# Column buffers and turned images in the second layer of a convolution-and-GRU kernel

## The chip, the cores and the metric

The kernel runs on one core of one Trainium2 chip. The metric is device time in microseconds of one execution; the time of the kernel before is the median of three runs, 5828.33 us (5819.98 to 5828.91). The core's engines are TensorE (PE in the profile, its weight loads PEld), VectorE (DVE), ScalarE (ACT), GpSimd (POOL) and SyncE (SP), which here only issues DMAs.

## The reference

Two layers, each added to its input, each on the group-normalized input (`_gn`, over 32 groups of channels):

```python
x = x + _L0_conv_ref(_gn(x), ...)   # 1x1 conv, depthwise 3x3, per-patch FFT product, layer norm, gate, 1x1 conv
x = x + _L1_conv_ref(_gn(x), ...)   # a GRU that walks over the columns of the image
```

All is float32, on a tensor of 4 images, 64 channels, 256 x 256 pixels. The change touches the second layer (layer 1) alone:

```python
f = jnp.transpose(features, (3, 0, 2, 1))            # columns first
def step(prev_col, cur_col):
    nb = jnp.concatenate([pad, prev_col, pad], axis=1)
    x = jnp.concatenate([nb[:, :-2], nb[:, 1:-1], nb[:, 2:]], axis=-1)   # three neighbours of the last new column
    new = _gru_cell(x, cur_col, w_ih, w_hh, b_ih, b_hh)                  # h = the old column
    return (new, new)
```

with r and z the sigmoids of the two gates, n = tanh(i_n + r * h_n), and the new column (1 - z) * n + z * h. Column 0 stays as it is; each of the 255 others needs the new column to its left, so the layer is a chain of 255 steps.

## The kernel before, in words

Layer 0 works block by block (32 blocks of 1024 patches), writes its result to a tensor in HBM (`x1`), and keeps its statistics on the chip. The change leaves its code alone. When its last store has landed, layer 1 begins.

In layer 1 a column of all four images is one tile of 128 partitions x 2 slots x 256 pixels: two images lie in the two halves of the partitions, two more in the second slot. The pairing of images with halves and slots differs between even and odd columns (`SLOTS`), because the matmuls of a step write the images into the other arrangement than the one that they read. An even column is one DMA, an odd one is two, one for each half.

- Loads. `load_columns(w)` (line 750) loads the columns w and w+1 by three DMAs on SP's queue, into `raw`, a tile of eight columns with three buffers (line 737). Sixteen columns are loaded ahead of the first step.
- Normalization. `normalize(w, slot)` (line 766) is an ACT instruction per slot that writes the normalized column into `xn`, a tile of eight columns with two buffers. The matmuls need two of the four images also in the other half of the partitions. After every second column, line 779 copies these from `xn` to `xt` by two DMAs from SBUF to SBUF on SP's queue. Nine columns are normalized ahead of the first step (line 877); step w then normalizes column w+8.
- A step. `column(w)` (line 819) cuts the 256 rows in two parts, whose border moves by one row per step and jumps back every 32 steps, so that part 0 of a step needs nothing of part 1 of the step before. For each part PE computes the gates into PSUM tiles: `pshr` (own column, then three taps of the last new column `st`), `pshn` (whole column, in part 0), `psni` (taps), `pshz` (own column and taps). `own` reads `xn` and `xt`. `state` (line 856) turns these into the new column: ACT makes g, z and n, DVE does five operations, of which the last writes `st`.
- Result. `add(w)` (line 785) is a GpSimd addition that puts the new column onto `raw` in place. After every second column three DMAs on SP's queue store both columns. Then three more load columns w+15 and w+16 (line 889).

The order on each engine is the order of the program (`InOrder`, lines 146 to 160); SP and GpSimd too work their queues in order. Tile pools put in the waits: a tile handed out again waits for all users of the buffer's last tile. Each DMA of SP takes one of eight completion semaphores in turn, and waits for the DMA that had it before.

Of the kernel before, what the change touches and what calls it, by code (L numbers as in the profile page):

```python
# [10 lines left out]
F32 = mybir.dt.float32  # L11
# [8 lines left out]
P = 128  # L20
# [143 lines left out]
def tile_conv_then_gru(  # L164
# [128 lines left out]
    with layer0 as s:  # L293
# [20 lines left out]
        def normalize(n, jq):  # L314

            t, b, at = xq[n, jq], n // 8, n % 8
            flat = t.rearrange("p j k -> p (j k)")
            shift, rstd = sc0[:, b, 0:1], sc0[:, b, 1:2]
            if jq == 3:
                nc.vector.tensor_scalar(flat, flat, rstd, shift, ALU.mult, ALU.add)  # L320
            else:
                nc.scalar.activation(flat, flat, AF.Identity, bias=shift, scale=rstd)
            grid = t.rearrange("p j (r c) -> p j r c", c=10)
            if jq % 2 == 0:
                nc.gpsimd.memset(grid[:, 0, :, 0:1], 0.0)
            else:
                nc.gpsimd.memset(grid[:, 15, :, 9:10], 0.0)
            if at == 0 and jq < 2:
                nc.gpsimd.memset(grid[0:C, :, 0, :], 0.0)
            if at == 7 and jq >= 2:  # L330
                nc.gpsimd.memset(grid[C:P, :, 9, :], 0.0)
# [402 lines left out]

    WB = 8
    with ExitStack() as s:
        rawp = s.enter_context(tc.tile_pool(name="raw", bufs=3))
        colp = s.enter_context(tc.tile_pool(name="cols", bufs=2))
        gk = s.enter_context(tc.tile_pool(name="gk", bufs=2))
        ps_g = s.enter_context(tc.tile_pool(name="ps_g", bufs=1, space=PSUM))  # L740
        raws, xns, xts, stcols = {}, {}, {}, {}

        def columns(m, w):

            yield m[:, :, w, :].rearrange("(k a) c h -> (a c) k h", k=NPAIR), slice(0, P), 0
            for half in range(2):
                b0 = SLOTS[1][0][half]
                yield m[b0 : b0 + 2, :, w + 1, :].rearrange("b c h -> c b h"), slice(half * C, half * C + C), 1

        def load_columns(w):  # L750
            n, i = w // WB, w % WB
            if i == 0:
                raws[n] = rawp.tile([P, 2, WB, H], F32, tag="raw", name=f"raw_{n}")
            for of, at, j in columns(x1, w):
                nc.sync.dma_start(raws[n][at, :, i + j], of)

        def new_columns(n):
            xns[n] = colp.tile([P, 2, WB, H], F32, tag="xn", name=f"xn_{n}")
            xts[n] = colp.tile([P, WB, H], F32, tag="xt", name=f"xt_{n}")

        def empty_states(n):
            stcols[n] = st = colp.tile([P, 2, WB, H + 2], F32, tag="st", name=f"st_{n}")
            nc.gpsimd.memset(st[:, :, :, 0:1], 0.0)
            nc.gpsimd.memset(st[:, :, :, H + 1 : H + 2], 0.0)

        def normalize(w, slot):
            n, i = w // WB, w % WB
            if i == slot == 0:
                new_columns(n)
            nc.scalar.activation(  # L770
                xns[n][:, slot, i],
                raws[n][:, slot, i],
                AF.Identity,
                bias=sc1[:, w % 2, slot, 0:1],
                scale=sc1[:, w % 2, slot, 1:2],
            )
            if slot and i % 2:

                for half in range(2):
                    nc.sync.dma_start(  # L780
                        xts[n][half * C : (half + 1) * C, i - 1 : i + 1],
                        xns[n][(1 - half) * C : (2 - half) * C, half, i - 1 : i + 1],
                    )

        def add(w):
            n, i = w // WB, w % WB
            nc.gpsimd.tensor_tensor(
                raws[n][:, :, i], raws[n][:, :, i], stcols[n][:, :, i, 1 : H + 1], ALU.add
            )
            if i % 2:  # L790
                for of, at, j in columns(out, w - 1):
                    nc.sync.dma_start(of, raws[n][at, :, i - 1 + j])

        QUARTERS = ((0, 0), (0, 1), (1, 0), (1, 1))
        SKEW = 32

        def parts(w):


            at = H // 2 + SKEW // 2 - (w - 1) % SKEW  # L800
            return (0, at), (at, H)

        MAX = H // 2 + SKEW // 2

        def bank_pair(gate, w):
            return ps_g.tile([P, 2, 512], F32, tag=gate, name=f"ps{gate}_{w}")

        def quarters(ps, weights, rhs, start, stop):
            for r, c in QUARTERS:
                nc.tensor.matmul(  # L810
                    ps[c * C : (c + 1) * C, r],
                    lhsT=weights[r * C : (r + 1) * C],
                    rhs=rhs(r, c),
                    start=start,
                    stop=stop,
                    tile_position=(r * C, c * C),
                )

        def column(w):

            i, xn, xt, st = w % WB, xns[w // WB], xts[w // WB], stcols[(w - 1) // WB]

            def own(ps, gate, h0, h1, stop):

                quarters(
                    ps,
                    wh[:, gate, :],
                    lambda r, c: (xn[:, c] if r == c else xt)[r * C : (r + 1) * C, i, h0:h1],
                    True,
                    stop,  # L830
                )

            def taps(ps, gate, h0, h1, start):
                for t in range(3):
                    quarters(
                        ps,
                        wi[:, 3 * gate + t, :],
                        lambda r, c: st[r * C : (r + 1) * C, c, (w - 1) % WB, h0 + t : h1 + t],
                        start and t == 0,
                        t == 2,  # L840
                    )

            pn = bank_pair("hn", w)[:, :, 0:H]
            for part in range(2):
                h0, h1 = parts(w)[part]
                pr, pi, pz = (bank_pair(gate, f"{w}_{part}")[:, :, 0 : h1 - h0] for gate in ("hr", "ni", "hz"))
                own(pr, 0, h0, h1, False)
                taps(pr, 0, h0, h1, False)
                if part == 0:
                    own(pn, 2, 0, H, True)  # L850
                taps(pi, 2, h0, h1, True)
                own(pz, 1, h0, h1, False)
                taps(pz, 1, h0, h1, False)
                state(w, part, pn[:, :, h0:h1], pr, pi, pz)

        def state(w, part, pn, pr, pi, pz):
            h0, h1 = parts(w)[part]
            i, num = w % WB, h1 - h0
            xn, st = xns[w // WB], stcols[w // WB]
            g = gk.tile([P, 2, MAX], F32, tag=f"g{part}", name=f"g_{w}_{part}")[:, :, 0:num]  # L860
            n = gk.tile([P, 2, MAX], F32, tag=f"n{part}", name=f"n_{w}_{part}")[:, :, 0:num]
            z = gk.tile([P, 2, MAX], F32, tag=f"z{part}", name=f"z_{w}_{part}")[:, :, 0:num]
            nc.scalar.activation(g, pr, AF.Sigmoid, bias=b_rz[:, 0:1], scale=1.0)
            if w + WB < W:
                normalize(w + WB, part)
            nc.vector.scalar_tensor_tensor(n, pn, bias_sb[:, 5:6], g, ALU.add, ALU.mult)
            nc.vector.tensor_tensor(n, pi, n, ALU.add)

            nc.scalar.activation(z, pz, AF.Sigmoid, bias=b_rz[:, 1:2], scale=-1.0)
            nc.scalar.activation(n, n, AF.Tanh, bias=bias_sb[:, 2:3], scale=1.0)  # L870
            nc.vector.scalar_tensor_tensor(g, z, -1.0, xn[:, :, i, h0:h1], ALU.add, ALU.mult)
            nc.vector.tensor_tensor(n, n, z, ALU.mult)
            nc.vector.tensor_tensor(st[:, :, i, 1 + h0 : 1 + h1], n, g, ALU.subtract)

        for w in range(0, 2 * WB, 2):
            load_columns(w)
        for w in range(WB + 1):
            for slot in range(2):
                normalize(w, slot)
        empty_states(0)  # L880
        nc.vector.tensor_copy(stcols[0][:, :, 0, 1 : H + 1], xns[0][:, :, 0])
        for w in range(W):
            n, i = w // WB, w % WB
            if i == 0 and n + 1 < W // WB:
                empty_states(n + 1)
            if w:
                column(w)
            add(w)
            if i % 2 and w + 2 * WB < W:
                load_columns(w + 2 * WB - 1)  # L890


# [59 lines left out]
```

## Time and profile before

| | before |
|---|---|
| median of the runs | 5828.33 us (5819.98 to 5828.91) |
| the profiled execution's own time | 5838.45 us |
| its span, first to last instruction | 5836.7 us, granted TensorE clock 0.993 |
| layer 0, from 0 to about 4303 us | PE busy 4069.9 us of 4303 |
| layer 1's steps, 4324 to 5830 us (1506 us) | PE busy 1401.2, PEld 1336.2, DVE 1059.7, ACT 906.5, POOL 306.8 us |
| DMA in this stretch | 41% of the time of 16 engines, 112 GB/s |

Layer 1 takes about a quarter of the time. Each row of the profile names the engine, the operation and the tiles that it writes and reads (out<-in); all rows carry line 158, the line of the helper through which each instruction is recorded, so the tiles are what to go by. Idle time is given with what ended it. "issue" there means that the profile shows no semaphore for which the engine waited. A busy PE isn't a PE at its peak, since matmuls overlap: the weight loads (PEld) show more sharply when PE's instruction stream stands still.

### The profile page before, as it was taken

The page shows a single profiled execution, that of the slowest core. Times are in us where ns is not written, and L with a number is a line of the kernel's source. Part 1 is how long each engine was busy: PE and PEld are TensorE (multiplying, and loading weights), DVE is VectorE, ACT ScalarE, POOL GpSimd, SP SyncE. Part 2 cuts the span into 40 slices and gives each one's busy share as a digit, 9 for nine tenths or more (in the row PEclk, how much of TensorE's full clock was granted, in tenths as well). Part 3 has the DMA queues.
Part 4 walks back from the last instruction along what each step waited for, and adds up shares of the span by engine and source line. Part 5 has one row for each costly group of instructions (what it writes and reads, how often), then busy time and mean ns, then how long its engine had stood idle before and what let it go on. Part 6 is the DMA issues. An engine that isn't in the chain of part 4 may idle for free. (4 is left out here: it accounts for less than half of the span.)

```text
span 5836.7 us, 278467 instructions
## 1 busy us (share of the span) xinstructions
PE 5472.7 (94%) x127204; PEld 4752.8 (81%) x127204; DVE 4076.5 (70%) x9593; ACT 3475.0 (60%) x4604; POOL 476.3 (8%) x749
## 2 busy tenths in 40 slices
PE   4999999999999999999999999999979999999998
PEld 3888888778878888888878888888768888888888
DVE  4777677777777777766777677666667776777766
ACT  3656666556566666556556666565556665666655
POOL 0000000000000000000000000000002221222212
PEclk9999999999999999999999999999989999999999
DMA  7555555555555555555555554544444444444443
GB/s 251 149 153 157 154 155 142 149 158 150 152 150 156 154 146 141 160 149 148 151 144 152 143 134 130 145 133 129 136 116 115 117 114 112 115 117 116 119 112 84
DMA packets 557274, 818.28 MB, mean 140 GB/s; under 512 B 37484, under 2 KB 431632, under 8 KB 553712
## 3 DMA queue, kind: packets, MB, share of 16 engines
q1 hardware_dynamic: 522256, 634.46, 40.4%
q0 software_dynamic: 33552, 165.43, 8.9%
q8 instruction: 996, 16.32, 1.2%
q14 instruction: 182, 1.49, 0.1%
q10 hardware_dynamic: 288, 0.58, 0.0%
HBM read 622.72 MB, written 144.05 MB: 131 GB/s over the span
## 5 line engine op out<-in xcount | busy, mean ns | idle before, releaser
L158 PEld LDWEIGHTS psring<-h,t 100*32 100x32 f32 x40960 | 1333.4, 115 | 303.9 <-issue 200.6
L158 PE MATMUL psring<-h,t 100*32 100x128 f32 x40960 | 1445.3, 274 | 115.3 <-issue 41.4
L158 PEld LDWEIGHTS psring<-w_sb,xq 64*100 64x100 f32 x24576 | 1355.8, 163 | 81.4 <-issue 51.1
L158 PE MATMUL psring<-w_sb,xq 64*100 64x128 f32 x24576 | 1399.9, 271 | 21.6 <-issue 7.6
L158 ACT COPY h<-psring 100x1024 f32<-100x1024 f32 x1274 | 1205.7, 1026 | 162.8 <-PE psring L158 154.4
L158 DVE TENSOR_TENSOR pr<-psring,q 128x512 f32<-128x512 f32 (+1 forms) x576 | 462.9, 857 | 336.5 <-PE psring L158 326.4
L158 DVE BATCH_NORM_STATS2 lnst<-z 128x6 f32<-128x64 f32 x4096 | 545.7, 216 | 117.6 <-ACT z L158 117.6
L158 DVE TENSOR_TENSOR z<-z,lnm 128x1024 f32<-128x1024 f32 x512 | 612.8, 1218 | 8.7
L158 ACT COPY q<-psring 128x1024 f32<-128x1024 f32 x256 | 259.3, 1013 | 527.4 <-PE psring L158 445.3
L158 ACT ACTIVATE z<-pshz,b_rz 128x288 f32<-128x288 f32 (+7 forms) x510 | 242.5, 476 | 520.6 <-PE pshz L158 520.6
L158 PE MATMUL pshr<-st,wi 64*64 64x144 f32 (+7 forms) x12240 | 511.2, 270 | 42.0 <-issue 26.1
L158 ACT COPY z<-psring 128x2048 f32<-128x2048 f32 x128 | 238.9, 1867 | 520.9 <-PE psring L158 520.9
L158 PE MATMUL pshz<-st,wi 64*64 64x144 f32 (+7 forms) x12240 | 513.0, 271 | 25.3 <-issue 24.0
L158 PE MATMUL psni<-st,wi 64*64 64x144 f32 (+7 forms) x12240 | 510.2, 270 | 21.0 <-issue 20.0
L158 PE MATMUL psring<-pr,g_sb 32*64 32x512 f32 x8192 | 488.7, 599 | 5.2 <-issue 5.1
L158 ACT ACTIVATE y<-psring,ln_sb 128x512 f32<-128x512 f32 x512 | 372.1, 780 | 201.5 <-PE psring L158 199.0
L158 PEld LDWEIGHTS psni<-st,wi 64*64 64x64 f32 x12240 | 447.1, 133 | 41.9 <-issue 30.1
L158 PEld LDWEIGHTS pshr<-st,wi 64*64 64x64 f32 x12240 | 422.2, 133 | 57.5 <-issue 54.8
L158 PEld LDWEIGHTS pshz<-st,wi 64*64 64x64 f32 x12240 | 427.0, 133 | 38.4 <-issue 37.7
L158 DVE COPY h<-psring 100x1024 f32<-100x1024 f32 x262 | 320.1, 1222 | 171.8 <-PE psring L158 167.9
L158 DVE SCALAR_TENSOR_TENSOR g<-z,xn 128x288 f32<-128x288 f32 (+7 forms) x510 | 218.4, 428 | 311.9 <-ACT z L158 310.3
L158 DVE TENSOR_TENSOR y<-psring,y 128x1024 f32<-128x1024 f32 x256 | 312.4, 1221 | 128.8 <-ACT y L158 127.9
(100 smaller groups left out, 7342.4 us busy)
## 6 DMA issues: line engine op xcount, KB each, us to landing
t<-t_all SPq DMA_DIRECT2D x768, 400.0 KB
xq<-in_xh POOLq DMA_DIRECT2D x128, 800.0 KB, 4.6
xr<-in_x SPq DMA_DIRECT2D x256, 256.0 KB
x<-xr SPq DMA_DIRECT2D x256, 256.0 KB
raw<-x SPq DMA_DIRECT2D x128, 256.0 KB
raw<-x SPq DMA_DIRECT2D x256, 128.0 KB
xt<-xn SPq DMA_DIRECT2D x256, 128.0 KB
out<-raw SPq DMA_DIRECT2D x128, 256.0 KB
```

The source lines that it names most:

```text
L158: return self.tc.keep_in_program_order(got(*args, **kwargs))
```

## The change

Columns get a buffer each: `raw` becomes a tile of one column with 16 buffers. After each step its column is stored at once, by one DMA (even) or two (odd), and one column is loaded, into the buffer that was just stored. The two images in `xt` are written by two GpSimd copies per column, in place of two DMAs per two columns. Four columns in place of nine are normalized ahead of the first step; steps 1 to 5 normalize two columns each, until the lead is eight columns as before.

```diff
-        rawp = s.enter_context(tc.tile_pool(name="raw", bufs=3))
+        rawp = s.enter_context(tc.tile_pool(name="raw", bufs=2 * WB))
...
-        def columns(m, w):
-
-            yield m[:, :, w, :].rearrange("(k a) c h -> (a c) k h", k=NPAIR), slice(0, P), 0
-            for half in range(2):
-                b0 = SLOTS[1][0][half]
-                yield m[b0 : b0 + 2, :, w + 1, :].rearrange("b c h -> c b h"), slice(half * C, half * C + C), 1
-
-        def load_columns(w):
-            n, i = w // WB, w % WB
-            if i == 0:
-                raws[n] = rawp.tile([P, 2, WB, H], F32, tag="raw", name=f"raw_{n}")
-            for of, at, j in columns(x1, w):
-                nc.sync.dma_start(raws[n][at, :, i + j], of)
+        def column_parts(m, w):
+
+            raw = raws[w]
+            if w % 2 == 0:
+                yield m[:, :, w, :].rearrange("(k a) c h -> (a c) k h", k=NPAIR), raw
+            else:
+                for half in range(2):
+                    b0 = SLOTS[1][0][half]
+                    yield m[b0 : b0 + 2, :, w, :].rearrange("b c h -> c b h"), raw[half * C : half * C + C]
+
+        def load_column(w):
+            raws[w] = rawp.tile([P, 2, H], F32, tag="raw", name=f"raw_{w}")
+            for of, to in column_parts(x1, w):
+                nc.sync.dma_start(to, of)
...
-                raws[n][:, slot, i],
+                raws[w][:, slot],
...
-            if slot and i % 2:
+            if slot:
 
                 for half in range(2):
-                    nc.sync.dma_start(
-                        xts[n][half * C : (half + 1) * C, i - 1 : i + 1],
-                        xns[n][(1 - half) * C : (2 - half) * C, half, i - 1 : i + 1],
+                    nc.gpsimd.tensor_copy(
+                        xts[n][half * C : (half + 1) * C, i], xns[n][(1 - half) * C : (2 - half) * C, half, i]
                     )
 
         def add(w):
-            n, i = w // WB, w % WB
-            nc.gpsimd.tensor_tensor(
-                raws[n][:, :, i], raws[n][:, :, i], stcols[n][:, :, i, 1 : H + 1], ALU.add
-            )
-            if i % 2:
-                for of, at, j in columns(out, w - 1):
-                    nc.sync.dma_start(of, raws[n][at, :, i - 1 + j])
+            nc.gpsimd.tensor_tensor(raws[w], raws[w], stcols[w // WB][:, :, w % WB, 1 : H + 1], ALU.add)
+            for to, of in column_parts(out, w):
+                nc.sync.dma_start(to, of)
...
-            if w + WB < W:
-                normalize(w + WB, part)
+            for more in range(ahead(w - 1), ahead(w)):
+                normalize(more, part)
...
-        for w in range(0, 2 * WB, 2):
-            load_columns(w)
-        for w in range(WB + 1):
+        def ahead(w):
+
+            return min(2 * w + 4, w + WB + 1, W)
+
+        for w in range(2 * WB):
+            load_column(w)
+        for w in range(ahead(0)):
             for slot in range(2):
                 normalize(w, slot)
...
         for w in range(W):
-            n, i = w // WB, w % WB
-            if i == 0 and n + 1 < W // WB:
-                empty_states(n + 1)
+            if w % WB == 0 and w + WB < W:
+                empty_states(w // WB + 1)
             if w:
                 column(w)
             add(w)
-            if i % 2 and w + 2 * WB < W:
-                load_columns(w + 2 * WB - 1)
+            if w + 2 * WB < W:
+                load_column(w + 2 * WB)
```

## The prediction

> **What bounds the kernel now.** The table of stretches comes first: layer 1's steps fill 1506 us, and PE is busy for 93% of them. The list of waits in that stretch says what the rest is.
>
> ```profile
> engine line waited for: us in total, times, longest us
> ...
> ACT z L158 <- PE pshz L158: 520.6, 510, 3.0
> ...
> PEld pshr L158 <- issue: 67.7, 95, 2.2
> ...
> PEld pshz L158 <- issue: 46.6, 76, 1.5
> ...
> PEld psni L158 <- issue: 30.1, 46, 1.5
> ...
> PE pshr L158 <- DVE st L158: 13.4, 7, 1.9
> ```
>
> ACT waits for PE, so PE sets the pace. PE itself waits for the recurrence (`st`) in 7 places alone, the jumps of the border. Its other pauses, 67.7 + 46.6 + 30.1 = 144 us, have no semaphore behind them. The chain of work shows them in the middle of a group of matmuls, here around 5242 us:
>
> ```profile
> 5241.77 0.47 PE psni L158 x16
> 5242.24 0.63 issue
> 5242.87 0.47 PE psni L158 x8
> ```
>
> The DMA table of the stretch says what comes in without a semaphore: instructions.
>
> ```profile
> q1 hardware_dynamic: 158638, 162.65, 39.6%
> q8 instruction: 366, 6.00, 1.7%
> ```
>
> 366 packets of 16,384 bytes in 1506 us, one per 4.1 us. I set these packets' records beside PE's and the data packets' records of the trace. A pause ends, nearly always, 1.2 to 1.6 us after such a packet has ended; the packet takes 1.06 us. Most of the difference between packets is in their start. Against the place in the instruction stream where the early ones start, it comes 0.2 to 0.3 us late where on average fewer than 8 data packets were in flight in the 1.5 us before, and 0.82 to 1.07 us late where 10 or more were. PEld's pause per packet is 0.16 us with fewer than 0.5 in flight, 0.20 to 0.34 with 2 to 10, and 0.66 to 0.76 with more; the mean is 0.42 us. With 366 packets that is 154 us. The last new column of a step follows the one before by 5.23 us in undisturbed steps and by 5.89 us in the mean: 0.66 x 254 = 168 us, nearly all of it instructions that come late, and about 15 us for the jumps.
>
> Where the dense data traffic comes from is in the timeline of SP's queue:
>
> ```profile
> 5226.00 1.89 SPq L158 DMA_DIRECT2D raw<-x  x3
> 5228.50 3.33 SPq L158 DMA_DIRECT2D xt<-xn  x2
> 5231.93 5.75 SPq L158 DMA_DIRECT2D out<-raw  x3
> 5237.73 1.88 SPq L158 DMA_DIRECT2D raw<-x  x3
> ```
>
> Every second step, the odd column's two stores and all three loads are issued back to back: 0.75 MB. The packet records show 10 to 15 data packets in flight for some 4 us then, another short stretch with the images' copies and the even column's store, and few in between.
>
> The start of layer 1 is bounded by another wait, in the timelines of SP and of PE:
>
> ```profile
> 4303.73 15.06 SPq L158 DMA_DIRECT2D raw<-x  x24
> 4318.89 8.70 SPq L158 DMA_DIRECT2D xt<-xn  x9
> ...
> 4323.07 1.31 PE L158 MATMUL pshr<-xt,wh 64*64 64x144 f32 x3 [13.31 <-DMA xt<-xn]
> ```
>
> The first image is turned by a DMA that stands on SP behind all 24 loads.
>
> [...] in this trace a store's last completion comes 2.4 to 4.1 us after its issue (median 2.56), worked out from its semaphore's updates. [...] The trace doesn't bear that out for the additions: 39 of the g<-z,xn operations overlap one, by 0.13 us, at 434 ns against 428 ns for the others. [...]
>
> **The change, part by part.**
>
> *Start.* PE needs st's borders, `xt` and `xn` of column 1. Loads are issued as before, so column 3's data is there at the same time, and the eight normalizations end where the eighth ended before, at 4311.4 (start 4307.0; the rows are 0.59 us long and follow by 0.5 us). Behind them on POOL stand the copies of column 3 and then four memsets of the borders, which move from 4299 to behind the copies (0.26 us for the four before). The taps wait for the memsets. A copy of 256 elements isn't in this trace. Bounds: the addition of 512 elements and two inputs takes 1185 ns, half of it is 0.59 us; [...] I take 0.45, two are 0.9. The taps start at 4311.4 + 0.9 + 0.3 = 4312.6, in place of 4324.0: 11.4 us gained. ACT's table load (1.28 us) then ends at 4312.7, before g is due. Bounds 9 to 13.
>
> *The ramp.* Steps 1 to 5 hold two more ACT instructions each, one per part, at 0.5 us. ACT waits 0.4 to 1.1 us for PE before z, which covers them; uncovered, it is 5 us in all. POOL then has four copies and an addition, 3.0 us of a step of 5.2. I take 0.
>
> *SP's queue.* Loads and stores stay three and three per two columns, with the same bytes. 256 issues of images (0.51 us each) and 32 MB go. New: a load waits on SP for the store just before it, for it takes its buffer. An even step costs SP 0.6 + 2.0 (wait for the receipt) + 0.6 = 3.2 us, an odd one 0.65 + 2.56 + 1.2 = 4.4; behind a waiting load stands the next step's store, which isn't due before 5.2 us. Loads run 16 columns ahead and are needed after 8 steps, 42 us, against 3.9 us from issue to landing. Cost 0.
>
> *DMA traffic.* The wait cuts the long stretch of stores and loads into four pieces of 256 KB per two steps, each some 1.1 to 1.5 us long (256 packets x 57 ns on 16 engines is 0.9 us at least) and 1 to 2 us apart. With these pieces over 10.9 us, the mean number of data packets in flight over 1.5 us never reaches 10. Weighing the pauses above by the new shares gives 0.25 us per packet in place of 0.42: 0.17 x 366 = 62 us. The class of 8 to 10 in flight, 24 packets, carries a quarter of that weight; at 0.45 us in place of 0.27 the gain is 47 us. I take 55. Ends: 0, if a dense microsecond delays as much as four, and 0.26 x 366 = 95, if only the idle pause of 0.16 us stays.
>
> *GpSimd.* 510 copies, 230 us on an engine that is busy for 307 of 1506 us. They follow ACT's second normalization, which ends after part 0's `st`; part 1's g is due about 1 us later. A pair of 0.9 us fits in between. If longer, it delays part 1's `st`, which in the middle is ready 0.95 us before PE asks for it. Cost 0; it is more from 1.95 us per pair. Every eighth step the borders' memset waits for PE on POOL ahead of the copies; images are made eight steps early.
>
> *End.* The last two stores were already issued by themselves after the last addition (4.4 us from last `st` to the last landing): 0.
>
> Sum: 11.4 + 55 = 66 us. The profiled execution of 5838.45 us (span 5836.7 and 1.75 around it) becomes 5772; it stands 10.1 us above the runs' median, which becomes 5828.3 - 66 = 5762. I predict 5763 us.
>
> **The rivals.**
>
> *The start alone.* Pauses depend on there being any dense traffic, not on its length, and the same bytes still flow. For: at 2 to 10 packets in flight the pause varies without order (0.20, 0.20, 0.34, 0.27). Against: it doubles above 10. Then 5828 - 11 = 5817 us.
>
> *Waits for instructions nearly all go.* 5828 - 11 - 95 = 5722 us. For: 84 packets in quiet traffic had 0.16 us. Against: with the pieces above, about nine of ten stretches of 1.5 us still touch one.
>
> *GpSimd's copies hold VectorE up.* The place is part 1's g, n and st. The slack is used up at 1.95 us per pair; each 0.1 us more costs 254 x 0.1 = 25 us, and from 2.2 us per pair the gain is gone. At 2.5 us it is 0.55 x 254 = 140, so 5762 + 140 = 5902 us. [...] Against: the addition, with twice the elements and two inputs, takes 1.19 us.
>
> *SP falls behind.* If the receipts of stores under load take 1.4 us more than 2.56, SP's mean of 3.8 us per step passes 5.2, the lead is eaten up, and the steps follow SP; at +0.3 us beyond, 5762 + 76 = 5838. Against: its quarter above 3.3 us stands in the denser traffic of before.
>
> **How the numbers follow.** The sum as worked out 0.62 (5740 to 5800), the start alone 0.16, instructions nearly free 0.10, GpSimd 0.08, SP 0.04. A measurement of this kernel can hardly tell less than 0.2%, 11.7 us, from no change, so the start alone stands on the border and is halved: faster 0.62 + 0.10 + 0.08 = 0.80, the same 0.08, slower 0.12. The range of 5728 to 5822 leaves out the slower cases and half of the nearly free one, 0.17.
>
> **What would show it.** PE's first wait of 13.31 us for `xt` falls to about 2 us behind POOL. The sum of PEld's "issue" waits in layer 1 falls from 144 to about 90 us; the row of instruction packets stays at 366. On SP's timeline stores and loads alternate with gaps of some 2 us. [...] Wrong is the prediction if PEld's "issue" sum stays, if DVE's g waits for POOL, or if ACT's xn waits for loads.

## The result, and the profile after

The changed kernel takes 5746.41 us (median of four runs, 5744.91 to 5753.36) against 5824.15 us for the kernel before (5813.40 to 5828.91; the three runs behind the 5828.33 us of the beginning, and a fourth): 78 us less. The ratio of the two is 0.9871, with a 95% interval of 0.9854 to 0.9889. The forecast was 5763 us, some 66 us less than before.

The profiled execution took 5743.0 us from first to last instruction, 93.7 less than the one before. It divides so, each time from the timelines of the two profiles:

| stretch | before | after | gain |
|---|---|---|---|
| layer 0, to SP's first load of a column | 4303.73 | 4290.79 | 12.9 |
| from that load to the first taps on PE | 20.27 | 8.36 | 11.9 |
| from the taps to the end of step 1 | 10.27 | 9.19 | 1.1 |
| the 254 steps after it | 254 x 5.885 = 1494.9 | 254 x 5.619 = 1427.1 | 67.7 |
| from the last `st` to the end | 7.56 | 7.52 | 0.0 |

Here the taps are PE's first matmuls on `st`. Layer 0 has the same code in both; its 12.9 us are a difference between two executions. In the fourteen profiled executions of this document, all with the same code there, SP's first load of a column lies anywhere from 4279.8 to 4308.9 us. The other rows make 80.8 us, which the medians bear out with 78. The repeat of the changed kernel below has 5.598 us per step where this profile has 5.619, a difference of 5 us over the steps.

In the steps the list of waits, for the stretch from the first taps to the last `st`, now has these for PE's weight loads:

```profile
engine line waited for: us in total, times, longest us
...
PEld pshz L158 <- issue: 27.1, 69, 1.7
PEld pshr L158 <- issue: 25.6, 62, 1.3
PEld psni L158 <- issue: 17.0, 43, 0.9
...
PEld pshr L158 <- DVE st L158: 15.7, 7, 2.2
```

The pauses without a semaphore have halved, from 144 to 69.7 us, where some 90 were forecast. They are read from the weight loads because the matmuls overlap: the 12,240 of pshr<-st, at 270 ns each, fill 531.9 us, and the matmuls' own "issue" pauses on these three tiles make 23.1 us. The recurrence still stops PE at the seven jumps of the border alone. The DMA table of the same stretch shows what is lighter:

```profile
q1 hardware_dynamic: 141167, 132.21, 31.8%
q8 instruction: 366, 6.00, 1.8%
```

The images' bytes are gone (162.65 to 132.21 MB), the 366 instruction packets are as many as before. PE's 46,912 matmuls and 46,912 weight loads in this stretch make 256 to a packet (46,916 of each and as many packets before). On SP's timeline the stores and loads now lie apart:

```profile
5143.03 1.34 SPq L158 DMA_DIRECT2D out<-raw  x2
5146.20 1.25 SPq L158 DMA_DIRECT2D raw<-x  x2
5148.38 0.38 SPq L158 DMA_DIRECT2D out<-raw  x1
5152.84 0.37 SPq L158 DMA_DIRECT2D raw<-x  x1
```

Between the end of a store's issue and the load's issue lie 1.8 to 4.1 us here. The start, on PE's timeline:

```profile
4296.22 0.95 PE L158 MATMUL pshr<-xt,wh 64*64 64x144 f32 x3
4296.68 0.50 PE L158 MATMUL pshr<-xn,wh 64*64 64x144 f32 x1
4296.97 0.44 PE L158 MATMUL pshr<-xt,wh 64*64 64x144 f32 x1
4296.98 0.44 PE L158 MATMUL pshr<-xn,wh 64*64 64x144 f32 x1
4299.15 1.72 PE L158 MATMUL pshr<-st,wi 64*64 64x144 f32 x24 [1.73 <-POOL st L158]
```

The wait of 13.31 us for the image's DMA has gone; the last wait before the taps is 1.73 us for the borders' memsets, behind the copies on POOL. And GpSimd's groups of instructions in the steps, with busy time and mean ns of one:

```profile
L158 POOL TENSOR_TENSOR raw<-raw,st 128x512 f32<-128x512 f32 x256 | 303.0, 1184 | 536.3 <-DVE st L158 399.5 <-ACT xn L158 114.2 <-POOL xt L158 14.1
L158 POOL COPY xt<-xn 64x256 f32<-64x256 f32 x504 | 208.6, 414 | 314.3 <-ACT xn L158 296.9
```

A copy takes 414 ns, so a pair 0.83 us, and POOL is busy for 516 of the 1437 us of this stretch.

### The profile page after: what moved, and what is told of

It is laid out like the page before. It is cut to its first block, busy times and chain, and to the rows that moved or that the text cites. A ratio compares the mean times of both kernels' runs of the same rounds, so it can differ in the third digit from the quotient of the medians.

```text
span 5743.0 us, 278945 instructions
## 1 busy us (share of the span) xinstructions
PE 5458.9 (95%) x127204; PEld 4737.3 (82%) x127204; DVE 4085.9 (71%) x9593; ACT 3473.2 (60%) x4604; POOL 687.9 (12%) x1261
## 5 line engine op out<-in xcount | busy, mean ns | idle before, releaser
L158 PE MATMUL pshr<-st,wi 64*64 64x144 f32 (+7 forms) x12240 | 531.9, 270 | 24.6 <-DVE st L158 13.8
L158 PE MATMUL pshz<-st,wi 64*64 64x144 f32 (+7 forms) x12240 | 533.4, 270 | 8.3 <-issue 6.2
L158 PE MATMUL psni<-st,wi 64*64 64x144 f32 (+7 forms) x12240 | 531.9, 270 | 6.8 <-issue 4.7
L158 PEld LDWEIGHTS psni<-st,wi 64*64 64x64 f32 x12240 | 459.6, 133 | 34.0 <-issue 17.0
L158 PEld LDWEIGHTS pshr<-st,wi 64*64 64x64 f32 x12240 | 441.3, 133 | 39.6 <-issue 20.3
L158 PEld LDWEIGHTS pshz<-st,wi 64*64 64x64 f32 x12240 | 448.0, 133 | 20.4 <-issue 19.7
```

The lines of the kernel that those rows point to most:

```text
L158: return self.tc.keep_in_program_order(got(*args, **kwargs))
```

## The experiments

The theory after the result is that of the prediction: PE's instructions come in packets that are late behind dense data traffic, and the change makes that traffic less dense by cutting the long stretch of stores and loads. Its rivals: that the 32 MB of images alone did it, that the start did most of it, and that something else than traffic holds the instructions up. Each kernel was timed beside the kernel before on the same chip; that one's medians there were 5827 us (first four runs), 5829 us (next four) and 5834 us (last four).

### Images by DMA again

Of the changed kernel; `w < 14` leaves the start to GpSimd.

```diff
-                    nc.gpsimd.tensor_copy(
-                        xts[n][half * C : (half + 1) * C, i], xns[n][(1 - half) * C : (2 - half) * C, half, i]
-                    )
+                    to, of = xts[n][half * C : (half + 1) * C, i], xns[n][(1 - half) * C : (2 - half) * C, half, i]
+                    if w < 14:
+                        nc.gpsimd.tensor_copy(to, of)
+                    else:
+                        nc.sync.dma_start(to, of)
```

> The changed kernel, but from column 14 on the two images of a column are again copied by DMAs on SP's queue, two of 64 KB per column; the start keeps GpSimd's copies. The image bytes (32 MB) are back, the stores and loads stay cut into pieces. Theory of the shape (PE's instructions come late behind long dense stretches of stores and loads): little lost, 5746 to 5766 us, PEld's issue waits in the steps (72 us in the changed kernel, 148 before) at 75 to 95. Rival of the bytes (it was the 32 MB of images that held instructions up): about 65 us lost, 5811 us, PEld's issue waits back at some 145.

Measured: 5887.67 us (5872.60 to 5904.81), ratio 1.0107 (1.0080 to 1.0134): slower than before, which neither side expected. SP's timeline and the list of SP's waits say why:

```profile
5136.42 0.53 SPq L158 DMA_DIRECT2D out<-raw  x1
5140.70 0.37 SPq L158 DMA_DIRECT2D raw<-x  x1
5141.11 1.11 SPq L158 DMA_DIRECT2D xt<-xn  x2
5142.32 1.33 SPq L158 DMA_DIRECT2D out<-raw  x2
5147.13 1.25 SPq L158 DMA_DIRECT2D raw<-x  x2
```

```profile
SPq L158 <- DMA out<-raw: 622.9, 240, 4.2
```

```profile
PEld pshz L158 <- ACT z L158: 127.5, 92, 3.0
PEld pshr L158 <- issue: 25.0, 28, 2.6
```

```profile
ACT xn L158 <- DMA raw<-x: 344.6, 178, 4.4
```

Of the 1561 us of the steps SP waits 622.9 for stores, and behind each of them a load and two images now stand in the queue. The loads come late: ACT's normalizations wait 344.6 us for them, where in the kernels before and after none does. PE then waits for ACT's z (the second list), since such a normalization stands ahead of z in ACT's program order. The steps take 6.15 us. This is the prediction's rival of SP falling behind, brought about by two more issues per step more than by slower stores (2.6 us of wait each, against 2.3 in the changed kernel). It says nothing of the images' bytes; for that the wait must go.

### The copies alone, in the kernel before

```diff
-            if slot and i % 2:
+            if slot:
 
                 for half in range(2):
-                    nc.sync.dma_start(
-                        xts[n][half * C : (half + 1) * C, i - 1 : i + 1],
-                        xns[n][(1 - half) * C : (2 - half) * C, half, i - 1 : i + 1],
+                    nc.gpsimd.tensor_copy(
+                        xts[n][half * C : (half + 1) * C, i], xns[n][(1 - half) * C : (2 - half) * C, half, i]
                     )
```

> The kernel before, with one edit: the images are made by GpSimd's copies. Blocks of eight columns, stores and loads in pairs, nine columns normalized first, as before. Theory of the shape: the long stretch of two stores and three loads is untouched, so the steps stay near 5.85 us; the start gains about 6 us, because the first image no longer stands behind 24 loads: 5804 to 5818 us. Rival of the bytes: the steps gain what the whole change gained, 5758 us.

Measured: 5795.29 us (5767.89 to 5800.72), ratio 0.9938 (0.9914 to 0.9961), so 32 us less than before on that chip. That is between the two: more than the start (in its profile the taps come 13.74 us after SP's first load, 6.5 us sooner than before), less than the whole. The pauses fall with the images' DMAs alone, from 144 to 81.9 us, in an execution that was the fastest of its kernel (5767.89 us):

```profile
PEld pshz L158 <- issue: 36.4, 60, 1.4
PEld pshr L158 <- issue: 26.2, 45, 1.7
PEld psni L158 <- issue: 19.3, 35, 1.4
```

So the images by DMA did hold instructions up. The prediction had no term for that.

### No wait between a store and the next load

```diff
-        rawp = s.enter_context(tc.tile_pool(name="raw", bufs=2 * WB))
+        rawp = s.enter_context(tc.tile_pool(name="raw", bufs=2 * WB + 4))
```

> The changed kernel with 20 column buffers in place of 16: a load takes a buffer that was stored four steps earlier, so it no longer waits on SP for the store just before it and follows it at once. Same bytes, same number of DMAs. Theory of the shape: store and load merge into one dense stretch of 512 KB per step, 2 us long; 20 to 40 us lost, 5766 to 5786 us, PEld's issue waits near 100. Rival (one column per step is enough, the wait does nothing): 5746 us within 10.

Measured: 5784.04 us (5758.30 to 5796.60), ratio 0.9940 (0.9917 to 0.9963), 38 us above the changed kernel by medians: the theory's value, at the upper end. SP's timeline shows the edit at work, and the list of waits its price, in an execution that was the fastest of its kernel (5758.30 us):

```profile
5142.94 0.38 SPq L158 DMA_DIRECT2D out<-raw  x1
5143.41 0.42 SPq L158 DMA_DIRECT2D raw<-x  x1
```

```profile
PEld pshz L158 <- issue: 36.4, 63, 1.5
PEld pshr L158 <- issue: 33.6, 63, 2.1
PEld psni L158 <- issue: 22.5, 51, 1.0
```

The load is issued 0.1 us behind the store, and the pauses rise from 69.7 to 92.5 us, with the same bytes and the same number of DMAs. The steps take 5.713 us against 5.619 and 5.598, which is 24 to 29 us in all. Waiting for a store made this kernel faster.

### No traffic in the steps

```diff
-            for to, of in column_parts(out, w):
-                nc.sync.dma_start(to, of)
+            if w >= W - 2 * WB:
+                for to, of in column_parts(out, w):
+                    nc.sync.dma_start(to, of)
...
-                load_column(w + 2 * WB)
+                raws[w + 2 * WB] = raws[w]
```

> The changed kernel without the loads of columns 16 to 255 and without the stores of columns 0 to 239; later columns work on the data of the sixteen first buffers, so most of the output isn't written. It bounds what data traffic costs in the steps. Theory of the shape: with no data packets each instruction packet still costs 0.16 us, so PEld's issue waits fall from 72 to 40 us or less and the time to about 5716 us. Rival (the pauses that are left have nothing to do with data traffic): 5746 us, PEld's issue waits unchanged.

Measured: 5705.00 us (5701.26 to 5713.22), ratio 0.9794 (0.9775 to 0.9813).

```profile
PEld pshr L158 <- DVE st L158: 15.9, 8, 2.2
PEld pshr L158 <- issue: 8.9, 29, 0.6
PEld pshz L158 <- issue: 7.5, 19, 0.6
PEld psni L158 <- issue: 7.1, 20, 1.6
```

The pauses fall to 23.5 us, the steps to 5.440 us. This is the bound: by the steps, data traffic costs 113 us in the kernel before and still 40 to 45 us in the changed one. Even at 8 GB/s of DMA traffic in the steps, against 97 in the changed kernel, PE still pauses behind instruction packets, by 0.11 us per packet.

### Images by DMA with 20 buffers

Both edits: images by DMA, and 20 buffers.

> As the run with images by DMA, but with 20 column buffers, so that a load doesn't wait for the store just before it: SP then issues for about 3 us per step and can't be the bound that the first of these runs showed. To be compared with the run of 20 buffers and GpSimd's copies (5784 us). If that bound was all that slowed the images by DMA: 5784 us and no waits of PE for ACT's z. If the 32 MB of images themselves hold up instructions, as the run of copies alone hints (29 us below before, of which 6 at the start): about 5807 us. If SP is still the bound: over 5850 us.

Measured: 5823.74 us (5812.54 to 5850.28), ratio 0.9990 (0.9979 to 1.0002): all of the gain is gone. SP isn't the bound any more: its list of waits has none for a store, where the first run with images by DMA had 622.9 us. The pauses are back where they were:

```profile
PEld pshr L158 <- issue: 62.4, 82, 2.2
PEld pshz L158 <- issue: 51.1, 73, 2.0
PEld psni L158 <- issue: 37.1, 56, 1.7
```

150.6 us, against 92.5 with GpSimd's copies and else the same code; the steps, at 5.901 us against 5.713, are 48 us longer in all. The 32 MB of images cost 40 us here by medians, 17 more than the 23 that were expected from the run of copies alone. Together with the runs above, as medians and, in brackets, as mean us per step after the first in the profiled execution, which leaves layer 0 and the start out:

| images | stores and loads in pairs | one column per step, no wait | with the wait |
|---|---|---|---|
| by DMA | 5824 to 5834, before (5.885) | 5824 (5.901) | 5888, SP is the bound (6.146) |
| by GpSimd | 5795 (5.728) | 5784 (5.713) | 5746, after (5.619) |

One column per step in place of two brings nothing by itself that could be told: 0 with the images by DMA, and with copies 11 us by medians but nothing by the ratios (0.9938 and 0.9940). By medians the images bring 29 to 40 us, the start included in the first, and the wait 38. By the steps, of which there is one execution each, the images bring 40 to 48 us and the wait 24, together the 67.7 us of the change.

### The start undone

```diff
-            return min(2 * w + 4, w + WB + 1, W)
+            return min(w + WB + 1, W)
```

> The changed kernel with nine columns normalized ahead of the first step, as before, and one per step from then on. Undoes the start alone. By the sum: the taps of the first step start 5.9 us later (ten more ACT instructions of 0.5 us and the copies behind them), steps 1 to 5 get back some 3 us: 5748 to 5752 us. Rival (the start is worth the whole 11.4 us, or the ramp costs as much as it brings): 5757 us, or 5746.

Measured: 5755.35 us (5731.29 to 5762.55), ratio 0.9867 (0.9838 to 0.9897): 9 us above the changed kernel by medians, but the scatter of its runs is 31 us and the interval takes in both sides. By the times the sum of 2 to 6 us is neither shown nor refuted; a loss of more than some 20 us is refuted. The profile leaves layer 0 out: the taps come 14.06 us after SP's first load in place of 8.36, 5.7 us later, and step 5 ends 44.8 us after that load against 41.7 in the changed kernel and 39.6 in its repeat. That is 3 to 5 us, as the sum has it.

### Each copy twice

The two lines of the copy stand twice, one behind the other.

> The changed kernel with each of GpSimd's copies made twice, the same values to the same place: a pair of 0.8 us becomes 1.6 us, GpSimd's share rises to about 3 us of a step of 5.6. By the sum nothing is lost below 1.95 us per pair: 5746 us, at most 10 more. Rival (GpSimd's copies hold VectorE up already, the added cover is gone): n<-n,z is 0.11 us longer where a copy overlaps it, so 20 to 60 us lost, 5766 to 5806 us.

Measured: 5741.07 us (5738.99 to 5758.29), ratio 0.9857 (0.9832 to 0.9881): nothing lost. GpSimd's groups show the doubled work:

```profile
L158 POOL COPY xt<-xn 64x256 f32<-64x256 f32 x1008 | 426.4, 423 | 313.9 <-ACT xn L158 267.1
```

218 us more on POOL move the time by nothing that can be told. The taps come 3 us later (11.45 us after SP's first load), since the memsets stand behind the doubled copies; the steps, at 5.567 us, are not longer. The rival of GpSimd holding VectorE up is out, for pairs up to 1.7 us.

### Even columns in two DMAs

```diff
-            if w % 2 == 0:
-                yield m[:, :, w, :].rearrange("(k a) c h -> (a c) k h", k=NPAIR), raw
-            else:
-                for half in range(2):
+            for half in range(2):
+                if w % 2 == 0:
+                    of = m[:, :, w, :].rearrange("(k a) c h -> a c k h", k=NPAIR)[half]
+                else:
                     b0 = SLOTS[1][0][half]
-                    yield m[b0 : b0 + 2, :, w, :].rearrange("b c h -> c b h"), raw[half * C : half * C + C]
+                    of = m[b0 : b0 + 2, :, w, :].rearrange("b c h -> c b h")
+                yield of, raw[half * C : half * C + C]
```

> The changed kernel with an even column stored and loaded by two DMAs of 64 partitions, as the odd ones are, in place of one of 128: the same bytes in pieces half as dense, 0.6 us apart, for two more issues on SP per two steps. Theory of the shape: fewer instruction packets behind a dense piece, 5 to 10 us gained, 5736 to 5741 us. Rival (pieces of 256 KB are short enough, or SP's issues and waits grow): 5746 us or above.

Measured: 5745.27 us (5739.52 to 5753.56), ratio 0.9858 (0.9833 to 0.9884): no gain that the runs show. The pieces didn't become less dense: the count of packets below, under why the prediction was right, shows more dense traffic here than in the changed kernel. Halving an even column's piece of 256 KB brought nothing here. Nor did the number of DMAs cost anything that could be told: 256 more of them, at 5745.27 us against 5746.41.

### The changed kernel again, the borders first, and half of the traffic

These four were timed together. First the changed kernel as it is.

> The changed kernel itself once more, beside the next three: how far its time moves from one chip and call to another. 5746 us within 10.

Measured: 5752.56 us (5744.36 to 5758.81), ratio 0.9859 (0.9840 to 0.9877), as in the first comparison (0.9871).

Then with `empty_states(0)` ahead of the loads:

```diff
+        empty_states(0)
         for w in range(2 * WB):
             load_column(w)
         for w in range(ahead(0)):
             for slot in range(2):
                 normalize(w, slot)
-        empty_states(0)
```

> The changed kernel with the borders' memsets of the first state block ahead of the loads and copies, where they were before the change, so that the first taps no longer wait for the copies of columns 2 and 3 on GpSimd. From the profile of the changed kernel: PE is through with the own column at 4297.4 and waits 1.73 us for the memsets; ACT's table load ends at 4299.75 in either case and the first g can't start before it, in place of 4300.93. So 1.2 us gained, 5745 us, not to be told from none. Rival (the wait for the memsets hides nothing else): the whole 1.7 us.

Measured: 5747.22 us (5728.56 to 5753.55), ratio 0.9845 (0.9822 to 0.9869), which can't be told from the changed kernel. PE no longer waits ahead of the taps, but ACT's table load is next, as expected: in this profile it runs from 4306.10 to 4307.38, and g starts at 4307.40, 9.3 us after SP's first load, against 10.1 us in the changed kernel (4300.93 after 4290.79). Step 1 ends 15.0 us after that load, against 17.6 and, in the repeat, 17.9: PE meanwhile went on with its other matmuls, and 2.6 us or more are gained, above either expectation. By the end of step 5 it is 39.4 us against 41.7 and 39.6. Nothing here beats the changed kernel by an amount that the runs show.

Then without the stores of columns 0 to 239 (the first part of the edit of the run without traffic), and without the loads of columns 16 to 255 (its second part).

> The changed kernel without the stores of columns 0 to 239, so that most of the output isn't written; loads as they are. Half of the traffic in the steps goes, and the load follows the addition without the wait for a store. With no traffic at all 41 us were gained. If only dense stretches that meet or follow each other closely hold up instructions, most of the 41 us goes with either half: 5710 to 5718 us. If each byte costs the same: 5725 us.

> The changed kernel without the loads of columns 16 to 255, which then work on the data of the sixteen first buffers, so the output isn't the reference's; stores as they are. If each byte costs the same: 5725 us. If it is the loads (reads of HBM) that hold up instructions: 5708 us here, and 5746 without the stores; if the stores, the other way round.

Measured: 5737.38 us (5730.02 to 5744.70) without the stores, ratio 0.9838 (0.9816 to 0.9860), and 5734.06 us (5725.92 to 5742.42) without the loads, ratio 0.9828 (0.9808 to 0.9848). Against 5752.56 that is 15 and 18 us, less than half each of the 41 us without both (38 by the two ratios, 0.9859 and 0.9794, of 5834). Neither carries it alone, and the idea that taking away either ends most of it isn't borne out. By the steps (5.559 and 5.500 us) the stores cost 10 to 15 us and the loads 25 to 30. Whether they differ is open: the intervals of the times overlap, and there is one profile of each.

## Why the prediction was right

**The bound, and what it costs.** PE's pauses without a semaphore follow instruction packets: right as far as these runs can show it. PEld's pause per packet, all its idle stretches that end between 0.8 and 2.0 us after a packet's end, falls from 0.43 to 0.26 us, where the sum had weighed out 0.25 in place of 0.42, and to 0.11 us with no traffic. Of the 47 to 62 us that followed, the prediction took 55. The steps gained 67.7 us.

The way to the 0.25 was in part luck. The prediction weighed by the data packets in flight in the 1.5 us before an instruction packet, and said that their mean would never reach 10. The packet records, counted so and also over 3 us, show this:

| kernel | 10 or more over 1.5 us: packets of 366, pause | 10 or more over 3 us: packets, pause |
|---|---|---|
| before | 151, 0.65 us | 85, 0.89 us |
| images by DMA, 20 buffers | 114, 0.48 us | 67, 0.92 us |
| copies, 20 buffers | 54, 0.35 us | 9, 0.40 us |
| even columns in two DMAs | 183, 0.29 us | 21, 0.19 us |
| changed kernel | 69, 0.33 us | 12, 0.31 us |

The mean does reach 10 in the changed kernel, for 69 packets, but they cost half of what such packets cost before. With even columns in two DMAs more packets meet that density than before the change, at 0.29 us. So the density of the last 1.5 us doesn't set the pause. What has gone is the packets behind stretches that stay dense for 3 us: before, 85 of them held 75 of 156 us of pauses, and now 12 hold 4 of 95. That count isn't the whole cause either, since in the run with even columns in two DMAs 21 such packets cost 0.19 us each. What in a stretch makes an instruction packet late is not shown.

**Why the traffic is less dense.** Here the prediction was right in part. It put its gain down to the wait that cuts the stretch of stores and loads; the going of the images' 32 MB stood under SP's queue, at cost 0. The runs give the wait 38 us by medians and 24 by the steps, the images 29 to 48. In the run with 20 buffers the images follow the loads at once on SP, and 67 instruction packets there stand behind 3 us of dense traffic, against 9 without them. So the images may act by the same mechanism, by making dense stretches longer, but no run moves their bytes into quiet time, and whether the bytes alone cost something stays open. That the sum came out near the measured gain is luck to this extent: its one term was sized for the whole of the thinner traffic and named after one of its two causes.

**The start.** 11.4 us were forecast, 11.9 measured from SP's first load to the first taps. The copies took 0.41 us each (0.45 taken, the author's estimate below the 0.59 us of half an addition). The ramp was taken at 0, right as far as the profiles show: from SP's first load to the end of step 5 it is 53.2 us before, 41.7 in the changed kernel and 39.6 in its repeat, so a gain of 11.5 us or more is still there when the ramp is over.

**SP's queue.** Cost 0, right: SP waits 560.7 us in 240 places for a store's completion (the prediction's receipt), 2.3 us each, where the prediction had 2.0 and 2.56, and no load is late (ACT's list of waits has none for a load). That this depends on the images leaving SP wasn't said; with them the loads come late, by 344.6 us of ACT's waits, and the kernel is slower than before by 60 us.

**GpSimd.** Cost 0, right, and not by luck: doubling it costs nothing that could be told (5741.07 us). A copy and n<-n,z both take longer where they overlap: n<-n,z takes 535 ns in the 73 places where a copy overlaps it, 426 ns elsewhere. The copies take 526 ns there, against 393 ns where they overlap none of VectorE's operations. The lengthening of n<-n,z by 0.11 us is less than the overlap of 0.25 us; what brings it about is not shown. Doubling the copies did not lengthen the steps, 5.567 us against 5.619.

**The rivals.** The start alone is out (the steps gained 67.7 us). Instructions nearly free, at 5722 us, is out for this kernel; without traffic, which it did not suppose, the time is 5705 us. SP falling behind did not happen in the change, and did in the first experiment.

## What to carry to other kernels

Where PE runs through its instructions as fast as here, 256 matmuls and weight loads per 4.1 us before, look for pauses named "issue" and set them beside the data traffic: bytes that needn't be moved by DMA, and stores and loads that go out back to back, cost PE time here although no instruction waited for them (40 and 38 us by medians). Look at how long the traffic stays dense too: half of the pauses before, 75 of 156 us, stood behind 3 us of it. A wait that only spaces out DMAs was a gain here, 5746 us against 5784, where the queue that waited had time to spare, and with the images' DMAs on that queue a loss, 5888 us against 5824; count the queue's issues and waits per step before adding to it. A small copy within SBUF was better done here by an engine with idle time than by DMA, 5784 us against 5824. And where a part of the kernel that didn't change differs between executions by as much as the effect, compare the changed part alone in the profiles.

## What the runs showed of the hardware

Waiting for a store's completion before the next load is issued made the kernel 38 us faster (5784 to 5746; 24 us by the steps of the profiles) at the same bytes and the same number of DMAs. DMAs from SBUF to SBUF of 64 KB, whose data PE uses only eight steps later, cost 40 us over the steps (5784 to 5824), while 256 more DMAs without more bytes cost nothing that could be told (5745). With 10 or more data packets in flight over the last 1.5 us PE's pause per instruction packet was 0.65 us in one kernel and 0.29 us in another; where that density had lasted 3 us, it was 0.89 and 0.19 us, for 85 and 21 packets. And without data traffic in the steps PE's instruction stream still paused for 23.5 us.
